# Gate and up products of up to five experts per batch as seven products over 64 channels

## Chip, cores, metric

One core of a Trainium2 chip runs the whole program. The metric is the device time of one execution in microseconds (us); lower is better. Engines: TensorE (PE, matmuls, with its weight loads as PEld), VectorE (DVE), ScalarE (ACT), GpSimd (POOL) and SyncE (SP, which here only issues DMAs). Each engine works through its own instructions strictly in program order and waits on semaphores for the others.

## What is computed

A block of linear attention and a block of eight dense experts, each between two layer norms with a residual, on 8 batches of 512 tokens with 128 channels, all in float32. The expert part is the larger one:

```python
x = x + _layernorm(attn(_layernorm(x), gamma, beta, w_qkv, w_out, b_out))
x = x + _layernorm(ffn(_layernorm(x), Wg, Wu, Wd))

def ffn(hidden, Wg, Wu, Wd):              # 8 experts, 128 channels, 512 inner
    x = hidden.reshape(-1, H)
    def expert_step(acc, w):
        wg, wu, wd = w
        h = silu(x @ wg) * (x @ wu)
        return acc + h @ wd, None
    acc, _ = scan(expert_step, zeros_like(x), (Wg, Wu, Wd))
```

## The kernel before

**Tiling of the experts.** The order of all work is written out by hand. For each batch `b` a list of units runs 32 steps; step `i` is block `f = i % 4` of 128 inner channels of expert `e = i // 4`. A step issues two matmuls, gate (L1164) and up (L1165): 128 input channels, 128 outputs, up to 512 tokens. A float32 matmul is two passes on PE, each with a weight load of its own. ACT takes the silu of the gate from PSUM (L1190), DVE multiplies it by up (L1196) into `h`. Two gate and two up banks of PSUM (`ps_gu`) take turns. All weights of gate, up and down are loaded once at the start and stay in SBUF (L116 to L125).

**Down-projection.** After the 32 steps `down_pairs` (L988) multiplies `h` with `wd`. Two blocks of 128 inner channels make a pair, two halves of the tokens and two halves of the outputs a 2x2 product that is done in Winograd's form with seven products instead of eight. `differences` (L978) makes the token-side terms of a pair on POOL with three instructions (L984 to L986); `weight_sums` (L966) makes the weight-side terms once. Each product has 64 output channels and is placed in one half of PE's columns, so two run side by side as column tiles (L1024), into the banks `accA` and `accB`. The pool `tp` has 10 buffers for `t`; the first 10 pairs get their differences during the steps, the last 6 during the down-projection.

**Around it.** `plan` (L1032) says at which step a piece of other work is issued, `meanwhile` (L1123) at which two pairs of the down-projection. While batch `b` is in its steps, the attention of batch `b+1` is finished (`context`, `values`, `stats3`, `scales3`, `residual`, `stats4`, `scales4`, `norm4`, `turn4`) and that of `b+2` begun (`load`, `stats`, `scales`, `norm`, `turn`, `affine`); `product` (L592) makes the keys of `b+2` (`k_ps`) just before the down-projection, and `softmax` follows in it. `scales` (L251) is a few small DVE instructions, then a power and a product on POOL. `turn` and `turn4` transpose blocks on DVE and pass them through DRAM (`carry_out`, one DMA; `carry_in`, four). The finished batch goes through `Last`: `turn` brings the two accumulators to tokens, `add` (L688) sums the seven products on DVE, `stats`, `scales` and `norm` make the last layer norm and store.

**Batch 0 and 7.** Batch 0 starts in pieces of one and two token blocks, so that PE has work early; its first 16 steps are run in two units. The last batch runs 24 steps whole and its last 8 in two halves with a plain down-projection, so that the end is short.

Of the kernel before, what the change touches and what calls it, by code (L numbers as in the profile page):

```python
# [9 lines left out]
F32 = mybir.dt.float32  # L10
# [6 lines left out]
def kernel(  # L17
# [60 lines left out]
    zp = ctx.enter_context(tc.tile_pool(name="zp", bufs=2))  # L78
    small = ctx.enter_context(tc.tile_pool(name="small", bufs=3))
    sgp = ctx.enter_context(tc.tile_pool(name="sgp", bufs=3))  # L80
    hp = ctx.enter_context(tc.tile_pool(name="hp", bufs=16))
    tp = ctx.enter_context(tc.tile_pool(name="tp", bufs=10))
    dram = ctx.enter_context(tc.tile_pool(name="dram", bufs=4, space=bass.MemoryType.DRAM))
    blk = ctx.enter_context(tc.tile_pool(name="blk", bufs=2))
    ps_gu = ctx.enter_context(tc.tile_pool(name="ps_gu", bufs=2, space=bass.MemoryType.PSUM))
    ps_acc = ctx.enter_context(tc.tile_pool(name="ps_acc", bufs=1, space=bass.MemoryType.PSUM))
    ps = ctx.enter_context(tc.tile_pool(name="ps", bufs=2, space=bass.MemoryType.PSUM))
# [27 lines left out]
    wg_sb, wu_sb, wd_sb = [], [], []  # L115
    for e in range(E):  # L116
        g = const.tile([P, F], F32, name=f"wg_{e}")
        nc.sync.dma_start(g, wg[e])
        u = const.tile([P, F], F32, name=f"wu_{e}")
        nc.sync.dma_start(u, wu[e])  # L120
        d = const.tile([P, NF, C], F32, name=f"wd_{e}")
        nc.sync.dma_start(d, wd[e].rearrange("(f p) c -> p f c", p=P))
        wg_sb.append(g)
        wu_sb.append(u)
        wd_sb.append(d)  # L125
# [206 lines left out]
    x2s, zTs, was, attentions, rest = {}, {}, {}, {}, []  # L332
# [225 lines left out]
    class Attention:  # L558
# [94 lines left out]
        def turn4(self):  # L653
            b = self.b
            zT = zp.tile([P, NQ, NJ, Q], F32, tag="zT", name=f"zT_{b}")
            to_channels(self.z, zT.rearrange("c a j i -> c a (j i)"), f"z_blk_{b}")
            zTs[b] = zT

    class Last:
# [28 lines left out]
        def add(self):  # L688
# [6 lines left out]
            nc.vector.tensor_tensor(u, p1, p6, ALU.add)  # L695
            nc.vector.tensor_tensor(c11, p1, p2, ALU.add)
            nc.vector.tensor_tensor(p4, p4, p4b, ALU.add)
            nc.vector.tensor_tensor(c21, u, p7, ALU.add)
            nc.vector.tensor_tensor(c12, u, p5, ALU.add)
            nc.vector.tensor_tensor(c22, c21, p5, ALU.add)  # L700
            both = q[:, 2:6].rearrange("p (s b) x -> p s b x", s=2)
            nc.vector.tensor_tensor(both, both, D[:, 0], ALU.add)
# [249 lines left out]
    LAG = 2  # L952
    FIRST = 16
    EARLY = 10
# [9 lines left out]
    ws_sb = [const.tile([P, NF // 2, 4, HALF], F32, name=f"ws_{e}") for e in range(E)]  # L964

    def weight_sums(engine, experts):  # L966

        for e in experts:
            w = wd_sb[e].rearrange("p (q k) c -> p q k c", k=2)
            a11, a21, a12, a22 = (w[:, :, k, c : c + HALF] for k in (0, 1) for c in (0, HALF))  # L970
            t = ws_sb[e]
            for i, (a, b, op) in enumerate((
                (a21, a22, ALU.add), (t[:, :, 0], a11, ALU.subtract), (a11, a21, ALU.subtract),
                (a12, t[:, :, 1], ALU.subtract),
            )):
                engine.tensor_tensor(t[:, :, i], a, b, op)

    def differences(pair):  # L978


        h = pair[0]
        t = tp.tile([P, 3, N // 2], F32, tag="t2", name="t2")
        pair.append(t)
        nc.gpsimd.tensor_tensor(t[:, 0:2], h[:, 1::2], h[:, 0:2], ALU.subtract)  # L984
        nc.gpsimd.tensor_tensor(t[:, 2], h[:, 3], t[:, 0], ALU.subtract)  # L985
        nc.gpsimd.tensor_tensor(h[:, 1], h[:, 2], t[:, 2], ALU.subtract)  # L986

    def down_pairs(b, pairs, calls):  # L988
# [4 lines left out]
        A, D = sums = [  # L993
            ps_acc.tile([P, N], F32, tag=f"acc{t}", name=f"acc{t}_{b}") for t in "AB"
        ]
        low, high = slice(0, HALF), slice(HALF, C)
        left, right = slice(0, N // 2), slice(N // 2, N)
        for two in range(0, len(pairs), 2):
            below, above = [], []
            for m, (h, t) in enumerate(pairs[two : two + 2]):  # L1000
                k = two + m
                e, pair = divmod(k, NF // 2)
                w0, w1 = wd_sb[e][:, 2 * pair], wd_sb[e][:, 2 * pair + 1]
                sm = ws_sb[e][:, pair]


                opens, closes = k == 0, k == len(pairs) - 1
# [3 lines left out]
                    (D[low, right], sm[:, 3], h[:, 3], opens, closes),  # L1011
# [3 lines left out]
                    (A[high, right], sm[:, 1], t[:, 2], opens, False),  # L1015
                    (D[high, left], sm[:, 2], t[:, 1], False, closes),
# [8 lines left out]
            late = EARLY + two // 2  # L1025
            if late < len(pairs):
                differences(pairs[late])
            for call in calls.get(two // 2, []):
                call()
        fins[b] = Last(b, sums)  # L1030

    def plan(b, lo, hi, begin):  # L1032
# [11 lines left out]
        def differ(k):  # L1044
            return lambda: differences(pairs[k])

        if b == B - 1 and begin:
            if not lo:
                at(24, lambda: fins[b].turn_both())
            else:  # L1050
                at(26, lambda: fins[b].add())
# [8 lines left out]
        elif b == 0 and begin < FIRST:  # L1060
# [8 lines left out]
            else:  # L1069
# [9 lines left out]
                for k in range(2):  # L1079
                    at(12 + 2 * k, differ(k))  # L1080
# [167 lines left out]
```

## Time and profile before

| what | us |
|---|---|
| median of 3 runs (683.97 to 684.29) | 684.22 |
| the profiled execution's span | 682.0 |
| one whole batch, 2 to 6 (183.01 to 265.78 and so on) | 82.77 |
| its down-projection (241.4 to 265.6) | 24.2 |
| POOL busy in one such batch | 52.8 |
| DVE busy in one such batch | 36.1 |
| ACT busy in one such batch | 30.7 |
| POOL busy from 241.6 to 265.7 (24.1) | 20.3 |

The span is what the profiler saw of one execution; the time of a run is 2.2 us more. A group's row gives line, engine, operation, output and inputs, shapes, the count, the busy time, the mean of one instruction in ns, and the idle time of the engine before them with what ended it. The chain of waits follows the work that ended last backwards, each time to what released it. In a timeline a row is start, length, engine, line, operation, and in brackets the idle time before it.

### The profile page before, as it was taken

The page shows a single profiled execution, that of the slowest core. Times are in us where ns is not written, and L with a number is a line of the kernel's source. Part 1 is how long each engine was busy: PE and PEld are TensorE (multiplying, and loading weights), DVE is VectorE, ACT ScalarE, POOL GpSimd, SP SyncE. Part 2 cuts the span into 40 slices and gives each one's busy share as a digit, 9 for nine tenths or more (in the row PEclk, how much of TensorE's full clock was granted, in tenths as well). Part 3 has the DMA queues.
Part 4 walks back from the last instruction along what each step waited for, and adds up shares of the span by engine and source line. Part 5 has one row for each costly group of instructions (what it writes and reads, how often), then busy time and mean ns, then how long its engine had stood idle before and what let it go on. Part 6 is the DMA issues. An engine that isn't in the chain of part 4 may idle for free.

```text
span 682.0 us, 9332 instructions
## 1 busy us (share of the span) xinstructions
PE 675.9 (99%) x3185; PEld 375.8 (55%) x3185; DVE 301.2 (44%) x806; ACT 249.3 (37%) x491; POOL 434.6 (64%) x543
## 2 busy tenths in 40 slices
PE   9999999999999999999999999999999999999997
PEld 7865565445654465544654446544465445644576
DVE  6756405554155441564325652356504545043425
ACT  5473332545035441344313443235412441033212
POOL 7599974775658576575855749557495583767501
PEclk9999999999999999999999999999999999999999
DMA  8511012010020111110111001201012000010020
GB/s 270 167 47 47 32 32 79 0 62 32 24 70 16 47 32 36 58 31 32 32 62 32 32 31 33 73 21 32 31 33 77 1 31 1 17 62 0 1 72 22
DMA packets 36815, 30.82 MB, mean 45 GB/s; under 512 B 4000, under 2 KB 28192, under 8 KB 36768
## 3 DMA queue, kind: packets, MB, share of 16 engines
q1 hardware_dynamic: 36192, 30.10, 13.8%
q8 instruction: 25, 0.41, 0.2%
q14 instruction: 22, 0.18, 0.1%
q10 hardware_dynamic: 576, 0.13, 0.1%
HBM read 18.42 MB, written 11.80 MB: 44 GB/s over the span
## 4 chain that ended last, share of the span: by engine, by line
PE 98%; DVE 0%; DMA 0%; POOL 0%; issue 0%; POOLq 0%; ACT 0%
PE g L1164 33%; PE u L1165 32%; PE accA L1024 16%; PE accB L1024 12%; PE y_ps L627 1%; PE g_ps L531 1%; PE k_ps L595 1%; PE end L905 1%; PE end_A L905 0%; DMA x<-in_L_attn_x_dram 0%; PE wa_ps L552 0%; PE m_ps L546 0%; PE c_ps L540 0%; PE end_B L905 0%; PE k_ps L397 0%; PE c_ps L432 0%
## 5 line engine op out<-in xcount | busy, mean ns | idle before, releaser
L1196 DVE TENSOR_TENSOR h<-sg,u 128x512 f32<-128x512 f32 (+2 forms) x268 | 172.9, 647 | 331.4 <-PE u L1165 310.6
L1190 ACT ACTIVATE sg<-g 128x512 f32<-128x512 f32 (+2 forms) x268 | 150.8, 564 | 338.0 <-PE g L1164 317.5
L1164 PE MATMUL g<-zT,wg 128*128 128x512 f32 (+2 forms) x568 | 267.3, 552 | 0.0
L1165 PE MATMUL u<-zT,wu 128*128 128x512 f32 (+2 forms) x568 | 266.2, 550 | 0.0
L984 POOL TENSOR_TENSOR t<-h 128x512 f32<-128x512 f32 x124 | 158.3, 1276 | 124.6 <-PE accB L1024 63.1
L1165 PEld LDWEIGHTS u<-zT,wu 128*128 128x128 f32 x568 | 107.3, 190 | 113.2 <-issue 109.3
L1164 PEld LDWEIGHTS g<-zT,wg 128*128 128x128 f32 x568 | 102.9, 190 | 95.6 <-issue 92.3
L1024 PE MATMUL accA<-h,wd 128*64 128x256 f32 x620 | 145.7, 380 | 0.0
L1024 PE MATMUL accB<-t,ws 128*64 128x256 f32 x496 | 137.8, 380 | 0.0
L1024 PEld LDWEIGHTS accA<-h,wd 128*64 128x64 f32 x620 | 84.3, 137 | 40.7 <-PE u L1165 3.8
L986 POOL TENSOR_TENSOR h<-h,t 128x256 f32<-128x256 f32 x124 | 90.8, 732 | 9.7
L985 POOL TENSOR_TENSOR t<-h,t 128x256 f32<-128x256 f32 x124 | 90.4, 729 | 9.7
L1024 PE MATMUL accA<-t,ws 128*64 128x256 f32 x248 | 73.8, 379 | 0.0
L1024 PE MATMUL accB<-h,ws 128*64 128x256 f32 x248 | 73.8, 379 | 0.0
L268 POOL TENSOR_TENSOR rstd<-ve,mhalf 128x4 f32<-128x4 f32 (+1 forms) x28 | 32.8, 1171 | 59.3 <-DVE nm L266 47.5
L1024 PEld LDWEIGHTS accB<-t,ws 128*64 128x64 f32 x496 | 67.3, 137 | 0.0
L1024 PEld LDWEIGHTS accB<-h,ws 128*64 128x64 f32 x248 | 34.0, 137 | 17.9
L1024 PE MATMUL accB<-h,wd 128*64 128x256 f32 x124 | 36.9, 379 | 0.0
L1024 PEld LDWEIGHTS accA<-t,ws 128*64 128x64 f32 x248 | 34.0, 137 | 0.0
L276 ACT ACTIVATE fn<-q,nm,rstd 128x128 f32<-128x128 f32 x28 | 11.5, 482 | 39.3 <-POOL nm L269 39.3
L276 ACT ACTIVATE x<-x,nm,rstd 128x128 f32<-128x128 f32 x56 | 22.9, 482 | 0.8 <-DVE z_blk L313 0.8
L1024 PEld LDWEIGHTS accB<-h,wd 128*64 128x64 f32 x124 | 17.0, 137 | 8.9
(207 smaller groups left out, 396.2 us busy)
## 6 DMA issues: line engine op xcount, KB each, us to landing
wg<-in_L_ffn_Wg_dram SPq DMA_DIRECT2D x8, 256.0 KB, 6.0
wu<-in_L_ffn_Wu_dram SPq DMA_DIRECT2D x8, 256.0 KB, 5.9
wd<-in_L_ffn_Wd_dram SPq DMA_DIRECT2D x8, 256.0 KB, 6.1
bounce<-f_blkA SPq DMA_DIRECT2D x8, 256.0 KB, 2.0
fA<-bounce SPq DMA_DIRECT2D x32, 64.0 KB, 2.0
bounce<-f_blkB SPq DMA_DIRECT2D x8, 256.0 KB, 2.2
fB<-bounce SPq DMA_DIRECT2D x32, 64.0 KB, 2.0
x<-in_L_attn_x_dram SPq DMA_DIRECT2D x7, 256.0 KB, 2.8
```

Of the source, the lines that this page charges most:

```text
L268: nc.gpsimd.tensor_tensor(rstd, ve, mhalf[:, :n], ALU.pow)
L276: nc.scalar.activation(d, t, AF.Identity, bias=nm[:, i : i + 1], scale=rstd[:, i : i + 1])
L531: nc.tensor.matmul(g_ps[:, :C], xh[:, j, :], ek[:, :, j * Q : (j + 1) * Q], start=(j == 0), stop=(j == NJ - 1),)
L595: nc.tensor.matmul(k_ps, w_qkv_sb[:, C : 2 * C], self.xnT, start=True, stop=True)
L984: nc.gpsimd.tensor_tensor(t[:, 0:2], h[:, 1::2], h[:, 0:2], ALU.subtract)
L985: nc.gpsimd.tensor_tensor(t[:, 2], h[:, 3], t[:, 0], ALU.subtract)
L986: nc.gpsimd.tensor_tensor(h[:, 1], h[:, 2], t[:, 2], ALU.subtract)
L1024: nc.tensor.matmul(o, w, r, start=start, stop=stop)
L1164: nc.tensor.matmul(g_ps[:, :cols], wg_sb[e][:, w], zT, start=True, stop=True)
L1165: nc.tensor.matmul(u_ps[:, :cols], wu_sb[e][:, w], zT, start=True, stop=True)
L1190: nc.scalar.activation(sg[:, :cols], g_ps[:, :cols], AF.Silu)
L1196: nc.vector.tensor_tensor(flat(h2)[:, first : first + cols], sg[:, :cols], u_ps[:, :cols], ALU.mult)
```

## The change

Experts 3 to 7 of batches 1 to 6 and experts 3 to 5 of batch 7 get gate and up by a 2x2 scheme of seven products. The 128 input channels are split in two halves of 64, the outputs (blocks `f` by twos) in two, the tokens in two halves. Gate and up are done side by side: one in rows 0 to 63 of PE, the other in rows 64 to 127 (`product`), each of 64 channels, 128 outputs and 256 tokens; a product is four such matmuls. The other experts keep the step of before.

- **Weights.** The weight-side terms are made once, in batch 0, by `start_forms` (four DMAs for each of two tiles), `form_chain` and `form_other` (three DVE instructions each, both operands in SBUF) and stored in DRAM (`forms`). Gate and up weights no longer stay in SBUF: `fetch` loads those of the next use into one of three buffers (512 KB, or 917 KB for a formed expert) when `done` says a buffer is read. `wd` is loaded in turn with them. `weight_sums` keeps three sums and overwrites a part of `wd`; the last batch loads `wd` of experts 6 and 7 again.
- **Tokens.** `turn4` writes the transposed tokens a second time, as `zd`, with eight more DMAs, so that both 64-channel halves lie in both halves of the partitions; `factors` makes the token-side terms with four DVE instructions at step 2.
- **PSUM.** One pool of four slots of two banks; `seven` uses slots 0 and 1, 2 and 3 by turns. Slot 3 is also the accumulator of the down-projection, slot 2 the attention's.
- **Between.** ACT copies three partial sums from PSUM, DVE adds, ACT takes four silus, POOL multiplies three quarters of `h` and DVE the fourth.
- **Order.** All attention work of a batch's steps is in its first 12 steps; `residual` and `stats4` to `turn4` are in the down-projection; `affine` stands behind `seven`. `add` of the last batch is on POOL, at step 5.
- **Down-projection.** It goes by quads (a whole expert). `tp` has four buffers of a quad's `t`; quads 0 and 1 get their differences at steps 6 and 10, 2 and 3 inside `seven`, 4 and 6 on POOL and 5 and 7 on DVE in the down-projection.

The core of the diff:

```diff
-    hp = ctx.enter_context(tc.tile_pool(name="hp", bufs=16))
-    tp = ctx.enter_context(tc.tile_pool(name="tp", bufs=10))
+    wp = ctx.enter_context(tc.tile_pool(name="wp", bufs=3))
+    hp = ctx.enter_context(tc.tile_pool(name="hp", bufs=8))
+    tp = ctx.enter_context(tc.tile_pool(name="tp", bufs=4))
...
+    slots = [psum.tile([P, 2, N], F32, name=f"s{k}") for k in range(4)]
...
+    def done(use):
+        del held[use]
+        fetch()
+        if wd_left:
+            fetch_wd(wd_left.pop(0))
...
+    def form_chain(e):
+        x = jobs[e][0]
+        a11, a21, a12, a22 = (columns(x, k, f) for k in (0, 1) for f in (0, 1))
+        nc.vector.tensor_tensor(a12, a21, a22, ALU.add)
+        nc.vector.tensor_tensor(a21, a11, a21, ALU.subtract)
+        nc.vector.tensor_tensor(a12, a12, a11, ALU.subtract)
+        nc.sync.dma_start(forms[e][:, : 2 * F].rearrange("p (k f) -> p k f", k=2), x)
...
+        def factors(self):
...
+            nc.vector.tensor_tensor(tz[:, 0], b22, b12, ALU.subtract)
+            nc.vector.tensor_tensor(b12, b12, b11, ALU.subtract)
+            nc.vector.tensor_tensor(tz[:, 1], b22, b12, ALU.subtract)
+            nc.vector.tensor_tensor(tz[:, 2], b21, tz[:, 1], ALU.subtract)
...
+    def differences(quad, engine=None):
+        h = quad[0]
+        t = tp.tile([P, 2, 3, N // 2], F32, tag="t4", name="t4")
+        quad.append(t)
+        sub = (engine or nc.gpsimd).tensor_tensor
+        return [
+            lambda: sub(t[:, :, 0:2], h[:, :, 1::2], h[:, :, 0:2], ALU.subtract),
+            lambda: sub(t[:, :, 2], h[:, :, 3], t[:, :, 0], ALU.subtract),
+            lambda: sub(h[:, :, 1], h[:, :, 2], t[:, :, 2], ALU.subtract),
+        ]
...
             for two_tiles in zip(below, above):
                 for o, w, r, start, stop in two_tiles:
                     nc.tensor.matmul(o, w, r, start=start, stop=stop)
-            late = EARLY + two // 2
-            if late < len(pairs):
-                differences(pairs[late])
-            for call in calls.get(two // 2, []):
+            if EARLY + e < len(quads):
+                differ(quads[EARLY + e], nc.vector if e % 2 else nc.gpsimd)
+            for call in calls.get(e, []):
                 call()
...
+        def product(bank, rows, weight, moving, start=False):
+            for q in range(2):
+                o = slice(q * N // 2, (q + 1) * N // 2)
+                for kind in sorted(range(2), key=lambda kind: rows[kind].start):
+                    r = rows[kind]
+                    nc.tensor.matmul(
+                        bank[:, kind, o], weight[r, q], moving[r], start=start and q == 0,
+                        stop=True, skip_group_check=True,
+                    )
...
+        for k, e in enumerate(experts):
+            x = Seven(k, e)
+            work7.append(x)
+            v = work7[k - 1] if k else None
+            u = work7[k - 2] if k > 1 else None
+            x.z1()
+            if v:
+                v.add22()
+            if u:
+                u.gate(u.c12)
+                u.up(u.c12, 1)
+                if k == 2:
+                    rest += differences(quads[FIRST_SEVEN])
+            x.w2()
+            x.take1()
+            if v:
+                v.z4()
+            x.add11()
+            if v:
+                v.gate(v.c22)
+                v.up(v.c22, 3)
+                v.gate21()
+            spare()
+            x.z6()
+            if v:
+                v.up21()
+            x.take6()
+            if v:
+                v.w3()
+                done(v.use)
+                v.add12()
+            x.w5()
+            x.gate(x.c11)
+            x.up(x.c11, 0)
+            spare()
+            x.z7()
+            x.take5()
+        v, u = work7[-1], work7[-2]
+        v.add22()
+        u.gate(u.c12)
+        u.up(u.c12, 1)
+        v.w3()
+        v.z4()
+        done(v.use)
+        v.gate(v.c22)
+        v.up(v.c22, 3)
+        v.add12()
+        v.gate21()
+        v.up21()
+        v.gate(v.c12)
+        v.up(v.c12, 1)
+        spare(len(rest))
...
             at(0, last("turn"))
             at(1, last("turn"))
+            at(2, attentions[b].factors)
...
+            at(5, last("add"))
             if b + 2 < B:
                 second = lambda name: lambda: getattr(attentions[b + 2], name)()
...
+                at(0, lambda: load(b + 2))
+                at(4, second("stats"))
+                at(5, second("scales"))
+                at(6, second("norm"))
+                at(8, second("turn"))
...
+            at(6, take_off(0))
+            at(10, take_off(1))
...
-        p[0] += last("add")
-        if b == 0:
-            first = attentions[1]
+        first = attentions.get(b + 1)
+        if first:
             p[0] += [first.residual]
-            p[1] += [first.stats4, first.scales4, first.norm4, first.turn4]
         if a:
             p[0] += [a.softmax]
+        if first:
+            p[1] += [first.stats4, first.scales4, first.norm4, first.turn4]
+        if b == 0:
+            for e, i in ((6, 0), (7, 3)):
+                p[i] += [partial(start_forms, e)]
+                p[i + 2] += [partial(form_chain, e), partial(form_other, e)]
         p[1] += last("stats") + last("scales")
...
         if whole:
+            if b:
+                calls = differences(quads[2])
+                experts = list(range(FIRST_SEVEN, end // NF))
+                seven(b, experts, quads, calls)
             if b + 2 < B:
+                if b:
+                    attentions[b + 2].affine()
                 attentions[b + 2].product()
-            down_pairs(b, pairs, meanwhile(b))
+            down_quads(b, quads, meanwhile(b))
```

In `seven`, `z1`, `z6`, `z7` and `z4` are products that add up in one slot, `w2`, `w5` and `w3` in the other; `take1`, `take6` and `take5` are ACT's copies of 2 x 512 elements, `add11`, `add12` and `add22` DVE's sums of a copy with a slot, `gate` the silu on ACT, `up` the product on POOL, `gate21` and `up21` the same straight from PSUM on ACT and DVE. `take_off` calls `differ` on POOL.

## Prediction

> **What bounds the kernel now.** I read the busy shares, then the chain of waits, then the groups kept apart by shape, then the timeline of one down-projection.
>
> ```profile
> PE 675.9 (99%) x3185; PEld 375.8 (55%) x3185; DVE 301.2 (44%) x806; ACT 249.3 (37%) x491; POOL 434.6 (64%) x543
> ...
> PE 98%; DVE 0%; DMA 0%; POOL 0%; issue 0%; POOLq 0%; ACT 0%
> ```
>
> TensorE (PE) is never idle and is the whole chain: PE work removed is time won, and any wait put on PE is time lost. Weight loads (PEld) lie under the matmuls. The other prices come from these groups (busy us, then mean ns of one):
>
> ```profile
> L1196 DVE TENSOR_TENSOR h<-sg,u 128x512 f32<-128x512 f32 x232 | 159.1, 687 | 322.0 <-PE u L1165 305.9 <-ACT sg L1190 16.1
> L984 POOL TENSOR_TENSOR t<-h 128x512 f32<-128x512 f32 x124 | 158.3, 1276 | 124.6 <-PE accB L1024 63.1 <-DVE h L1196 61.5
> L1190 ACT ACTIVATE sg<-g 128x512 f32<-128x512 f32 x232 | 138.0, 595 | 327.5 <-PE g L1164 307.3 <-DVE mv L257 20.1
> L985 POOL TENSOR_TENSOR t<-h,t 128x256 f32<-128x256 f32 x124 | 90.4, 729 | 9.7
> L1196 DVE TENSOR_TENSOR h<-sg,u 128x256 f32<-128x256 f32 x28 | 11.6, 419 | 8.8 <-PE u L1165 4.7 <-ACT sg L1190 3.2 <-PE z_ps L292 0.4
> L1190 ACT ACTIVATE sg<-g 128x256 f32<-128x256 f32 x28 | 10.6, 381 | 9.2 <-PE g L1164 9.0
> ```
>
> From 256 to 512 elements ACT grows by 214 ns, DVE by 268, POOL by 547; carried on to 1024 elements (estimates) ACT takes 1.02 us, DVE 1.22, POOL 2.37.
>
> PE in the down-projection of batch 2, two column tiles side by side:
>
> ```profile
> 330.25 0.14 PEld L1024 LDWEIGHTS accA<-h,wd 128*64 128x64 f32 x1
> 330.26 0.14 PEld L1024 LDWEIGHTS accB<-t,ws 128*64 128x64 f32 x1
> 330.47 0.14 PEld L1024 LDWEIGHTS accA<-h,wd 128*64 128x64 f32 x1
> 330.47 0.14 PEld L1024 LDWEIGHTS accA<-t,ws 128*64 128x64 f32 x1
> ```
>
> Both tiles load at one moment, and a new pair of passes starts every 0.216 us. Last, VectorE (DVE) and POOL where both work from SBUF, at one batch's end:
>
> ```profile
> 242.91 0.28 DVE L699 TENSOR_TENSOR q<-q,fB 128x128 f32<-128x128 f32 x1
> 243.11 1.37 DVE L700 TENSOR_TENSOR q<-q,fB 128x128 f32<-128x128 f32 x1
> 244.51 0.91 DVE L702 TENSOR_TENSOR q<-q,fB 128x256 f32<-128x256 f32 x1
> ```
>
> ```profile
> 242.99 1.33 POOL L984 TENSOR_TENSOR t<-h 128x512 f32<-128x512 f32 x1 [9.26 <-PE accB L1024]
> 244.40 0.73 POOL L985 TENSOR_TENSOR t<-h,t 128x256 f32<-128x256 f32 x1
> 245.21 0.79 POOL L986 TENSOR_TENSOR h<-h,t 128x256 f32<-128x256 f32 x1
> ```
>
> L700 has the shape of L699 and takes 1.37 us for 0.28: it ends when POOL's L984 does. A DVE instruction with two SBUF operands waits for POOL's running one. L1196, one operand in PSUM, does not.
>
> **The products (-27.4).** One step of `f` (two full matmuls, 512 columns) is four passes of 0.43 us, 1.72; an expert is 6.88. The new expert is 28 matmuls of 64 rows and 256 columns, two passes each, two row tiles at once: 28 pairs of passes. Row tiles are not in the trace. Nearest row: the column tiles' 0.216 a pair; upper bound: two 128-column weight loads one after the other, 2 x 0.190 (mean of L1164's loads) = 0.38. I take 0.216, as one 0.190 load fits under it: 6.05 an expert, 0.83 saved. Five experts in batches 1 to 6 and three in batch 7 are 33: 27.4 us.
>
> [...] The column tiles here reach 98% of the full array's rate, which is why I hold to the row.
>
> **Inside seven (+14.3).** Per expert ACT has three 1024-element copies and four gates, 5.4 us; DVE three adds and one product, 4.35; POOL three products, 3.8: each under 6.05. The tightest loop is w5, take5, add22, next z4, z6, w3, w5: 0.20 (PE's stream to ACT's start, 293.16 to 293.36) + 1.02 + 0.03 + 1.22 + 0.1 + four products of 0.864 = 6.03. It just fits; I take no stall (bounds 0 and 0.2 an expert). At the start nothing lies between: z6 waits for take1 (0.45), w5 for add11 (0.39), z7 for take6 (0.07), the next z4 for add22 (0.28). At the end only w3 lies between z7 and the last z4: add22 ends 1.61 after z7, z4 starts at 1.71, not 0.86: 0.85. Together 2.04 a batch, seven times.
>
> **Tile modes (+1.2).** From column tiles to the full array the next matmul starts 0.1 late (265.40 to 265.71 where 0.215 is usual). Two more changes in batches 1 to 5, one in 6 and 7: 12 x 0.1.
>
> **The key product (+11.5).** `affine` moves from step 30 to behind `seven`. It is last in ACT's queue: after z4 ends, gate21 (0.20 + 0.60), gate c12 (0.60) and affine itself (L583, 0.80) must pass before k_ps, 0.1 later. PE, with down_quads queued behind k_ps, idles 2.3 us, in batches 1 to 5.
>
> **Steps 0 to 11 (+2).** They now hold the attention of both later batches. ACT's norm at step 6 waits for the 8-column power (1.64) of step 5; that delays a gate so that step 9 waits some 0.4 us; five times. Upper bound 2 each. The fetches (917 KB for an expert of seven) have three experts' time, 18 us; at the 289 GB/s of the first 24.7 us one takes 3.2.
>
> **Quad 6 (+49.8).** This decides. Count from the first down matmul; each quad is 3.02 us of PE (the steps of the chain), so quad 6 is wanted at 18.1. `tp` has four buffers, so quad 4's differences wait for quad 0's products: POOL starts at 2.8 and needs 5.0 (2.37 + 1.28 + 1.28 and gaps). Behind it in POOL's queue lie the residual sum (1.27), the power and product of scales4, those of the last batch's scales, and only then quad 6. DVE holds quad 5's differences (three two-operand SBUF instructions), stats4, the transpose of turn4, then the last batch's stats.
>
> With DVE and POOL running on without holding each other: quad 4 7.8, residual 9.07, stats4 and its aggregates 10.6, power and product 11.9, four norms 13.6, transpose 14.3, last stats 15.75, their power 17.0, quad 6 17.05 to 22.05: 4.0 late. With each two-operand DVE instruction waiting for POOL's and POOL's for it: residual 10.65, stats4 begins at 11.3, power and product 14.05, transpose 16.5, power and product 19.2, then quad 7's DVE work and quad 6 by turns, to 26.4: 8.3 late. The rows show DVE waiting in full and POOL by 0.06 behind instructions of 0.28; how far POOL waits behind one of 1.22 they don't show. I take the upper end, since L986's 0.79 for 0.73 is a wait too: 8.3 in batches 1 to 6.
>
> [...]
>
> **The clock (+11.4).** The granted clock halves 2.7 us after PE's last matmul (at 680.2; the last ends at 677.5), and the first ten matmuls take 603 ns for 381. A stall of 8.3 us reaches that; restarting took some 4 us, so about 1.9 us are lost. Six times; bounds 0 and 3.4 each.
>
> **Batch 0 (+5).** Forms of experts 3 to 5: six two-operand DVE instructions each, 0.42 plus a wait of about 0.7 behind POOL, in two steps of 1.72; three PSUM pairs cover some 2.7 of the delay; I take 3 in all. Those of 6 and 7 fall beside quads 6 and 7: 2. Bounds 0 and 10.
>
> **Covered.** Formed weights' stores, the eight added DMAs for `zd` (0.35 to issue each; landed near 25, the next batch starts after 32), reloads of wd: all under PE's products. If down ran its bare 24.2 us, `zd` would come about 1 us after the batch's start, before step 2 needs it.
>
> **Sum.** -27.4 + 14.3 + 1.2 + 11.5 + 2 + 49.8 + 11.4 + 5 = +67.8. On the profiled span of 682.0: 749.8; the median lies 2.2 above the span, so 752.
>
> **Rivals.** *Queue without lock*: quad 6 waits only for its place in POOL's queue, 4.0; 25.8 less, and 3 less in batch 0: 723. For it: POOL's rows are hardly lengthened. Against: DVE's are, by a factor of five. *Quad 6 in time* (the other side): the rows of scales leave POOL free before 13.1, so that its 5.0 end by 18.1; that point decides. Quad 6, the clock, batch 0 and steps 0 to 11 then cost nothing: -0.4, 683.8, no slower, and faster if the border waits are shorter as well. Against: the chain residual to transpose took 6.5 us in batch 0 (81.6 to 88.1), and it can't start before quad 4 is through. *Weight loads in turn*: 0.38 a pair, 10.64 an expert, 4.6 x 33 more: about 900. Against: the paired loads above.
>
> **Chances.** Forecast 0.55, lock-free queue 0.25, quad 6 in time 0.12 (0.07 faster, 0.02 same, 0.03 slower), loads in turn 0.05, else 0.03. A change under 0.2% can't be told from none here. Faster 0.08, same 0.03, slower 0.89. The lowest bounds of clock, batch 0 and steps with the 4.0 give 708; the highest of all these, the loop's 0.2 an expert too, 781; a little of the third case and of a PE pass over 0.216 widens this to 700 and 785.
>
> **What would show it.** PE passes in `seven` every 0.216; PE idle before k_ps of 2.3 us with affine as releaser; PE idle before quad 6 of 4 to 9 us released by POOL, with the clock dropping there; DVE differences far over 1.2 us. If quad 6's wait is missing, or quad passes are well over 0.216, the forecast is wrong.

## The result, and the profile after

The changed kernel takes 841.89 us (median of 4 runs, 839.55 to 842.12), the one before 684.25 on the same chip: a ratio of 1.2297, interval 1.228 to 1.2314. The forecast was 752, with 700 to 785 as its range: the side was right, the size was off by 90 us. The profiled execution took 839.55, its span is 837.7 us (before 682.0): 155.7 more, where the terms summed to 67.8.

First the busy shares, the chain of waits and the granted clock, from the page of the changed kernel:

```profile
PE 719.7 (86%) x4505; PEld 462.4 (55%) x4505; DVE 423.5 (51%) x860; ACT 345.5 (41%) x590; POOL 495.0 (59%) x460
...
PEclk9998898999989999999989999899998999899999
...
PE 61%; DVE 19%; POOL 7%; ACT 6%; issue 3%; DMA 2%; SPq 1%; DVEq 0%; ACTq 0%; POOLq 0%
```

PE was 99% busy and 98% of the chain; now it idles for 118 us, and DVE holds 19% of the chain, more than POOL, at which the forecast looked. The groups by shape say where:

```profile
L1445 PE MATMUL s<-zT,w 128*128 128x512 f32 x200 | 113.0, 647 | 54.7 <-DVE h L1477 54.2
...
L1141 PE MATMUL s<-t,ws 128*64 128x256 f32 x496 | 150.1, 407 | 22.9 <-POOL t L1099 22.2 <-DVE t L1099 0.7
L1162 PE MATMUL s<-zd,w 64*128 64x256 f32 x1056 | 128.3, 380 | 3.0 <-ACT s L1203 2.1
L1162 PE MATMUL s<-tz,w 64*128 64x256 f32 x792 | 102.5, 388 | 2.6 <-ACT s L1203 1.7
```

The last column is the idle time before the group and who ended it. The new row-tile matmuls (L1162) wait for hardly anything. Quad 6 (POOL's L1099) costs 22.2 us of waiting. The largest wait, 54.2 us, stands before the gate matmul of the plain steps (L1445) and is ended by DVE's product `h` (L1477); no term of the forecast has it. With the shorter shapes of batches 0 and 7 it is 63.6 us on the page; some 45 of these are 58 waits of 0.6 to 0.9 us, and 7.46 and 4.45 are two waits for the weight sums (below). On the page of the kernel before, the gate matmul waits for nothing:

```profile
L1164 PE MATMUL g<-zT,wg 128*128 128x512 f32 (+2 forms) x568 | 267.3, 552 | 0.0
```

The same by stage, from the starts of PE's stages in the timeline. Before, a whole batch of 82.77 us is 24.2 of down-projection, 0.86 of key product, 34.4 for 20 steps of 1.72, and so 23.3 for the first 12 steps with the attention's products.

| part | forecast, us | measured, us |
|---|---|---|
| batch 0 (100.2 to 133.0) | +5 | +32.9 |
| steps 0 to 11 of batches 1 to 6 (194.9 against 6 x 23.3) | +2 | +55.1 |
| seven and key product there (213.1 against 6 x 34.4 + 5 x 0.86) | -0.1 | +2.4 |
| down-projection there: quad 6 and clock (192.7 against 6 x 24.2) | +61.2 | +47.5 |
| batch 7 (103.9 against 86.1) | -0.4 | +17.8 |
| sum | +67.7 | +155.7 |

The rows of forecast are the prediction's terms: -24.9 + 12.2 + 1.1 + 11.5 for `seven` and the key product of batches 1 to 6, 49.8 + 11.4 for the down-projection, and -2.5 + 2.0 + 0.1 for batch 7.

Of the steps' 55.1 some 7.5 are a wait of batch 1 for the weight sums (below). Batch 1's down-projection and batch 2's steps 0 to 11 as windows (length; busy us and count of PE, PEld, DVE, ACT, POOL; granted clock; DMA share; GB/s):

```profile
208.60:242.00 33.40, 29.49 (x225) 18.48 (x224) 12.42 (x30) 8.50 (x17) 18.89 (x16) 0.85 0.18 56
242.04:273.07 31.03, 25.61 (x72) 11.54 (x71) 15.81 (x45) 8.10 (x15) 11.80 (x15) 1.00 0.36 115
```

```profile
242.04 1.12 PE L1445 MATMUL s<-zT,w 128*128 128x512 f32 x2
243.00 1.02 PE L1446 MATMUL s<-zT,w 128*128 128x512 f32 x2
243.20 0.60 ACT L1471 ACTIVATE sg<-s 128x512 f32<-128x512 f32 x1 [10.08 <-PE s L1445]
244.13 0.69 DVE L1477 TENSOR_TENSOR h<-sg,s 128x512 f32<-128x512 f32 x1 [14.05 <-PE s L1446]
...
244.88 1.12 PE L1445 MATMUL s<-zT,w 128*128 128x512 f32 x2 [0.85 <-DVE h L1477]
```

In the first window PE idles 3.9 us and runs at 0.85 of its clock; in the second the clock is full and 5.4 us are idle. The second fence shows rows of the first step there and the gate of the next. Gate runs from 242.04, up from 243.00, ACT's silu and DVE's product follow, and the next step's gate starts only when that product has ended: 2.84 us for a step of 1.72, although two gate and two up banks are there.

### The profile page after: what moved, and what is told of

It reads as the page before. It is cut to its first block, busy times and chain, and to the rows that moved or that the text cites. A ratio compares the mean times of both kernels' runs of the same rounds, so it can differ in the third digit from the quotient of the medians.

```text
span 837.7 us, 12135 instructions
## 1 busy us (share of the span) xinstructions
PE 719.7 (86%) x4505; PEld 462.4 (55%) x4505; DVE 423.5 (51%) x860; ACT 345.5 (41%) x590; POOL 495.0 (59%) x460
## 3 DMA queue, kind: packets, MB, share of 16 engines
q1 hardware_dynamic: 63520, 88.57, 33.4%
## 4 chain that ended last, share of the span: by engine, by line
PE 61%; DVE 19%; POOL 7%; ACT 6%; issue 3%; DMA 2%; SPq 1%; DVEq 0%; ACTq 0%; POOLq 0%
PE s L1162 22%; PE s L1141 13%; PE s L1445 13%; PE s L1446 10%; DVE h L1477 6%; POOL rstd L352 3%; DVE t L1099 2%; ACT s L1203 2%; POOL t L1099 2%; DVE t L1100 1%; DVE h L1101 1%; ACT z L360 1%; DVE stats L332 1%; DMA Y<-in_L_ffn_Wg_dram 1%; DVE s L1216 1%
## 5 line engine op out<-in xcount | busy, mean ns | idle before, releaser
L1445 PE MATMUL s<-zT,w 128*128 128x512 f32 (+2 forms) x304 | 145.4, 560 | 67.7 <-DVE h L1477 63.6
L1477 DVE TENSOR_TENSOR h<-sg,s 128x512 f32<-128x512 f32 (+2 forms) x136 | 82.6, 608 | 220.3 <-PE s L1446 176.5
L1141 PE MATMUL s<-h,wd 128*64 128x256 f32 x744 | 188.3, 401 | 0.0
L1141 PE MATMUL s<-t,ws 128*64 128x256 f32 x496 | 150.1, 407 | 22.9 <-POOL t L1099 22.2
L1446 PE MATMUL s<-zT,w 128*128 128x512 f32 (+2 forms) x304 | 133.6, 522 | 0.0
L1162 PE MATMUL s<-zd,w 64*128 64x256 f32 x1056 | 128.3, 380 | 3.0 <-ACT s L1203 2.1
L1099 POOL TENSOR_TENSOR t<-h 128x1024 f32<-128x1024 f32 x47 | 111.0, 2361 | 32.1 <-PE s L1141 27.6
L1141 PEld LDWEIGHTS s<-h,wd 128*64 128x64 f32 x744 | 104.7, 145 | 44.8 <-issue 6.2
L1445 PEld LDWEIGHTS s<-zT,w 128*128 128x128 f32 x304 | 48.5, 191 | 127.4 <-DVE h L1477 104.7
L1162 PEld LDWEIGHTS s<-zd,w 64*128 64x128 f32 x1056 | 100.5, 187 | 24.7 <-issue 5.3
L1162 PE MATMUL s<-tz,w 64*128 64x256 f32 x792 | 102.5, 388 | 2.6 <-ACT s L1203 1.7
L1229 POOL TENSOR_TENSOR h<-s 128x512 f32<-128x512 f32 x66 | 84.3, 1278 | 13.9 <-ACT s L1225 12.9
L1446 PEld LDWEIGHTS s<-zT,w 128*128 128x128 f32 x304 | 58.0, 193 | 51.8 <-issue 49.3
L1162 PEld LDWEIGHTS s<-tz,w 64*128 64x128 f32 x792 | 72.7, 186 | 23.1 <-DVE s L1222 10.1
```

Of the source, the lines that this page charges most:

```text
L1099: lambda: sub(t[:, :, 0:2], h[:, :, 1::2], h[:, :, 0:2], ALU.subtract),
L1141: nc.tensor.matmul(o, w, r, start=start, stop=stop)
L1162: nc.tensor.matmul(bank[:, kind, o], weight[r, q], moving[r], start=start and q == 0, stop=True, skip_group_check=True,)
L1229: nc.gpsimd.tensor_tensor(self.h[:, :, i], c[:, 0], c[:, 1], ALU.mult)
L1445: nc.tensor.matmul(g_ps[:, :cols], wt[:, :F][:, w], zT, start=True, stop=True)
L1446: nc.tensor.matmul(u_ps[:, :cols], wt[:, F : 2 * F][:, w], zT, start=True, stop=True)
```

## The experiments

Theory after this: the 0.85 us are a wait for a PSUM slot. `Banks` hands out halves of slots that are one tile of two banks, and the two counters `g` and `u` are out of step by one when the whole steps begin, so that gate of step i+1 lies in the slot whose other half holds up of step i; a wait is kept for the tile, not for its half. Rival: it is the silu's buffers, of which the changed kernel has two for three. Beside this the forecast's own steps are tried: quad 6 and the holding between DVE and POOL, the key product, the weight sums.

**e1_phase: gate and up of a step in one slot.**

```diff
-    ps_gu = Banks(g=[(0, 0), (1, 0)], u=[(0, 1), (1, 1)])
+    ps_gu = Banks(g=[(0, 0), (1, 0)], u=[(1, 1), (0, 1)])
```

> The two places of the bank list for up are swapped, so that gate and up of a step lie in one slot. Theory (gate of step i+1 lies in the slot that holds up of step i, and waits until DVE has read that): the 0.85 us waits of PE behind DVE's product in steps 0 to 11 vanish, 31.0 us of steps in batch 2 become about 24, and the time falls by 7 x 7 us and some of batch 0: 780 to 795. Rival (two buffers for the gate's silu where there were three, or DVE's load in these steps): the waits stay, 842.

Measured 797.7 us, 44 less for one exchange of two pairs. Rows of the first step of batch 2 in e1, with the gate of the next:

```profile
221.55 1.13 PE L1445 MATMUL s<-zT,w 128*128 128x512 f32 x2
222.51 1.02 PE L1446 MATMUL s<-zT,w 128*128 128x512 f32 x2
223.37 1.02 PE L1445 MATMUL s<-zT,w 128*128 128x512 f32 x2
223.57 0.60 ACT L1471 ACTIVATE sg<-s 128x512 f32<-128x512 f32 x1 [10.85 <-PE s L1446]
224.20 0.69 DVE L1477 TENSOR_TENSOR h<-sg,s 128x512 f32<-128x512 f32 x1 [14.52 <-ACT sg L1471]
```

The next gate starts at 223.37, before the silu. The tile's wait is still there, but it now falls on ACT, which waits for up (L1446) instead of gate and has time for it. The changed kernel's two silu buffers are untouched here, so they don't make the wait either. By stage, batch 0 is 15.0 us shorter and batch 7 12.2, steps 0 to 11 of batches 1 and 6 13.0 together, but those of batches 2 to 5 only 0.7 to 1.1 each, where the theory had 7. There a second wait came up behind the first, here in batch 2:

```profile
236.75 0.46 POOL L809 TENSOR_TENSOR fB<-fB,fA 128x128 f32<-128x128 f32 x1 [3.76 <-DMA fB<-bounce]
...
239.20 1.65 POOL L352 TENSOR_TENSOR rstd<-ve,mhalf 128x8 f32<-128x8 f32 x1
...
241.16 1.65 ACT L360 ACTIVATE xh<-x,nm,rstd 128x128 f32<-128x128 f32 x4 [5.36 <-POOL nm L353]
...
244.07 1.22 PE L1445 MATMUL s<-zT,w 128*128 128x512 f32 x1 [4.34 <-DVE h L1477]
```

`add` of the last batch waits in POOL's queue for its transfer; the power of `scales` stands behind it, ACT's `norm` waits for that, the silu stands behind `norm`, and PE loses 4.3 us.

**e5_phase_order: e1, and `stats` and `scales` ahead of that `add`.**

```diff
-                at(4, second("stats"))
-                at(5, second("scales"))
+                at(3, second("stats"))
+                at(4, second("scales"))
```

> The bank order of the first experiment, and statistics and scales of the next but one batch one step earlier (3 and 4), so that their power stands before the sums of the last batch in POOL's queue. Theory (the one 4 us wait left in steps 0 to 11 is ACT's norm at step 6, which waits for a power that stands in POOL's queue behind sums that wait for a DMA): that wait vanishes in batches 1 to 5, the steps of batch 2 take about 24.5 us instead of 30.3, and the time falls from 797.7 to 770 to 778. Rival (ACT or DVE are short of time there whatever the order): 790 to 798.

775.45 us. Steps 0 to 11 of batch 2 fall from 31.0 to 24.5 (219.6 to 244.1). Both together win 66.4 us. In steps 0 to 11 of batches 1 to 6 they take 41.9 of the 55.1 away; 5.6 of what is left is batch 1's wait for the weight sums.

**e7_before_two_buffers: the rival with the silu's buffers, on the kernel before.**

```diff
-    sgp = ctx.enter_context(tc.tile_pool(name="sgp", bufs=3))
+    sgp = ctx.enter_context(tc.tile_pool(name="sgp", bufs=2))
```

> The kernel before, with two buffers for the gate's silu instead of three. Theory (the waits of the steps come from PSUM slots, not from these buffers): no change, 683.5 to 685.5. Rival (two buffers alone make PE wait behind DVE's product): over 690.

684.65 us against 684.37: with e1, that rival is out.

**e2_late_scales: quad 6 ahead of the last batch's power.**

```diff
-        p[1] += last("stats") + last("scales")
+        p[3] += last("stats") + last("scales")
```

> Statistics and scales of the batch before are issued after quad 7's differences instead of after the transpose of turn4. Theory (quad 6 waits for its place in POOL's queue behind their power): quad 6's differences begin right after the product of scales4, some 7 us earlier; the down-projection of batches 1 to 6 takes 25 to 28 us instead of 33.4, with no clock drop; 842 becomes 800 to 815. Rival (quad 6 waits for its buffer, or for DVE's sums alone): 835 to 845.

803.85 us, as the theory said. The down-projection of batch 1 takes 25.1 us instead of 33.4, and PE waits 0.52 in it. So quad 6's place in POOL's queue is the cause of its wait, and 38 us hang on it.

**e6_psum_operand: DVE's differences with one operand from PSUM.**

```diff
+        if engine is nc.vector:
+            p = slots[0].rearrange("p a (b x) -> p a b x", b=2)
+            return [
+                lambda: sub(t[:, :, 0:2], h[:, :, 1::2], p, ALU.subtract),
+                lambda: sub(t[:, :, 2], h[:, :, 3], p[:, :, 0], ALU.subtract),
+                lambda: sub(h[:, :, 1], h[:, :, 2], p[:, :, 0], ALU.subtract),
+            ]
```

> The changed kernel, with one operand of DVE's differences (quads 5 and 7, and as many in batch 7) taken from an idle PSUM bank of the same shape, so those terms are something else; all lengths, orders and waits stay. Theory (a DVE instruction with two SBUF operands and a POOL instruction hold each other up): DVE's three take 1.22, 0.69 and 0.69 us everywhere, POOL's third instruction of quad 4 takes 1.28 instead of 2.13 and the residual sum 1.27 instead of 1.71, quad 6 is ready 3 to 4 us sooner, and 842 becomes 815 to 825. Rival (POOL is slow there by itself, or DVE waits for something else): POOL's instructions stay as long, 838 to 842.

The terms that DVE makes are something else in this run. 815.5 us: 26 us go with the holding between DVE and POOL. The 38 of e2 and these 26 overlap, since both shorten the same wait for quad 6; they don't add up. Timeline of the changed kernel in batch 1: on DVE two differences of quad 5 and the first of quad 7, on POOL the last two of quad 4, the residual, the last batch's power and the first of quad 6:

```profile
215.90 1.87 DVE L1099 TENSOR_TENSOR t<-h 128x1024 f32<-128x1024 f32 x1 [3.56 <-PE s L1141]
217.80 1.65 DVE L1100 TENSOR_TENSOR t<-h,t 128x512 f32<-128x512 f32 x1
...
227.42 1.22 DVE L1099 TENSOR_TENSOR t<-h 128x1024 f32<-128x1024 f32 x1
...
215.42 1.27 POOL L1100 TENSOR_TENSOR t<-h,t 128x512 f32<-128x512 f32 x1
216.77 2.13 POOL L1101 TENSOR_TENSOR h<-h,t 128x512 f32<-128x512 f32 x1
218.86 1.71 POOL L728 TENSOR_TENSOR x<-x,x 128x512 f32<-128x512 f32 x1
...
227.52 1.98 POOL L352 TENSOR_TENSOR rstd<-ve,mhalf 128x4 f32<-128x4 f32 x1 [3.75 <-DVE nm L350]
...
230.10 2.34 POOL L1099 TENSOR_TENSOR t<-h 128x1024 f32<-128x1024 f32 x1
```

The same instructions in e6:

```profile
215.66 1.22 DVE L1101 TENSOR_TENSOR t<-h,s 128x1024 f32<-128x1024 f32 x1 [3.80 <-PE s L1148]
216.80 0.68 DVE L1102 TENSOR_TENSOR t<-h,s 128x512 f32<-128x512 f32 x1
...
216.53 1.28 POOL L1108 TENSOR_TENSOR h<-h,t 128x512 f32<-128x512 f32 x1
217.77 1.26 POOL L728 TENSOR_TENSOR x<-x,x 128x512 f32<-128x512 f32 x1
...
225.54 1.01 POOL L352 TENSOR_TENSOR rstd<-ve,mhalf 128x4 f32<-128x4 f32 x1 [3.74 <-DVE nm L350]
...
226.78 2.36 POOL L1106 TENSOR_TENSOR t<-h 128x1024 f32<-128x1024 f32 x1
```

Same lengths of data, one operand moved out of SBUF: DVE's second difference falls from 1.65 to 0.68 us, POOL's third from 2.13 to 1.28, and the power from 1.98 to 1.01. At 227.42 and 227.52 of the changed kernel it is DVE that holds POOL: DVE's L1099 begins first, has its 1.22, and POOL's power of 1.02 begun 0.10 later ends at 229.50, 0.86 after DVE. The holding goes both ways, and a small power pays for a large difference.

**e3_early_affine: `affine` at the first expert of `seven`.**

```diff
+            if not v and b + 2 < B:
+                attentions[b + 2].affine()
...
-                if b:
-                    attentions[b + 2].affine()
```

> affine of the next but one batch is issued after the first take1 of seven instead of behind it. Theory (PE idles before the key product for ACT's queue alone): the 1.97 us of idle time before the key product vanish in batches 1 to 5, and nothing else moves: 842 becomes 830 to 834. Rival (the idle time only moves, as the down-projection still waits for quad 6): 840 to 842.

824.88 us, 17 less, and 5 below the range expected. The wait before the key product is gone (1.97 to 1.98 in every batch of the changed kernel, released by L670), which is 2.0 in each of five batches; the down-projections are 0.5 to 1.8 shorter besides. Part of that is the clock: in the changed kernel's batch 1 the window from the key product on is the first row below, with 0.60 granted; in e3 it is the second, with 1.00:

```profile
207.33:211.60 4.27, 4.27 (x18) 2.02 (x20) 0.72 (x2) 3.54 (x7) 0.59 (x1) 0.60 0.20 73
208.14:212.41 4.27, 4.27 (x34) 2.50 (x34) 1.37 (x3) 4.07 (x8) 2.41 (x3) 1.00 0.41 123
```

The rest was not traced further.

**e4_no_form_sums: the changed kernel without the weight-side sums.**

```diff
-        nc.vector.tensor_tensor(a12, a21, a22, ALU.add)
-        nc.vector.tensor_tensor(a21, a11, a21, ALU.subtract)
-        nc.vector.tensor_tensor(a12, a12, a11, ALU.subtract)
...
-        nc.vector.tensor_tensor(a21, a21, a22, ALU.add)
-        nc.vector.tensor_tensor(a11, a21, a11, ALU.subtract)
-        nc.vector.tensor_tensor(a11, a12, a11, ALU.subtract)
```

> The sums of form_chain and form_other are left out (the weights are stored as loaded, so the experts of seven compute something else); loads and stores stay. Theory (DVE's two-operand instructions wait for POOL and for their loads at the head of DVE's queue, and the steps' products wait behind them): batch 0 ends 12 to 18 us earlier, among it the 7.5 us at the start of batch 1; 842 becomes 824 to 830. Rival (batch 0 is long because of the weights' loads or the opening): 838 to 842.

In this run the experts of `seven` compute something else. 831.09 us, 1 above the range expected. Batch 1 begins 9.5 us earlier (123.5 for 133.0); some of it is lost again to other waits in batch 1. What the sums look like in the changed kernel, DVE's timeline in batch 0 and at the start of batch 1, where the sums that were issued at the end of batch 0's down-projection stand:

```profile
74.78 1.50 DVE L196 TENSOR_TENSOR X<-X 128x256 f32<-128x256 f32 x1 [2.95 <-DMA X<-in_L_ffn_Wu_dram]
76.32 1.37 DVE L197 TENSOR_TENSOR X<-X 128x256 f32<-128x256 f32 x1
77.61 1.48 DVE L198 TENSOR_TENSOR X<-X 128x256 f32<-128x256 f32 x1
79.01 0.67 DVE L1477 TENSOR_TENSOR h<-sg,s 128x512 f32<-128x512 f32 x1
...
138.37 0.43 DVE L196 TENSOR_TENSOR X<-X 128x256 f32<-128x256 f32 x1 [7.41 <-DMA X<-in_L_ffn_Wu_dram]
```

Three sums of 0.42 take 4.2 us, since each waits for POOL's running instruction (those end at 76.01, 77.40 and 78.80, the sums at 76.28, 77.69 and 79.09), and a step's product (L1477) stands behind them. Those of expert 7 are worse: they stand in DVE's queue 7.4 us before their load is there, and batch 1's first product waits behind them; PE idles 7.46 us.

**e8_combined, e9_combined_more: all waits at once.** e8 is e5 with `affine` as in e3, `scales` as in e2, the key product between the last `w3` and `z4`, and the residual to `turn4` ahead of the first quad. e9 adds: `x` loaded at the end of the down-projection instead of at step 0 behind it, `affine` at the second expert, the residual in the epilog of `seven`, and the key maximum behind `seven`. The core of e9:

```diff
+            if k == 1 and b + 2 < B:
+                attentions[b + 2].affine()
...
+        if b + 1 < B:
+            attentions[b + 1].residual()
...
         v.w3()
+        if b + 2 < B:
+            attentions[b + 2].keys_product()
         v.z4()
...
-            p[1] += [first.stats4, first.scales4, first.norm4, first.turn4]
+            p[-1] += [first.norm4, first.turn4]
...
-        p[1] += last("stats") + last("scales")
+        p[3] += last("stats") + last("scales")
```

> The bank order, the step order of the first run of this set, affine after the first take1 and the key product between the last w3 and z4 of seven, residual to turn4 issued ahead of the first down quad, and statistics of the last batch behind quad 7's differences. Theory (these four waits are all that the batches lose): a whole batch takes 81 to 83 us instead of 99, the clock stays full from batch 2 on, and the time is 700 to 712, what is left being batch 0's forms and the opening. Rival (the row tiles or ACT, DVE and POOL inside seven cost more than PE's products, or new waits take their place): 725 or more.

> The combined kernel with the tokens of the next batches loaded at the end of the down-projection instead of at step 0, affine in the second expert of seven, the residual's norm at the end of seven, and the key maximum behind seven. Theory (the whole batch of 84.0 us in the combined run still holds the wait of the statistics for x, that of ACT for affine's tokens, and a late residual): a whole batch takes 80.5 to 82 us, and the time is 705 to 716. Rival (what is left is the price of the seven products themselves): 720 to 726.

e8 takes 724.49 us, between theory and rival; e9 712.44. A whole batch of e9 takes 81.9 us:

```profile
234.04:315.90 81.86, 80.88 (x577) 53.73 (x576) 53.14 (x96) 44.87 (x72) 63.42 (x55) 1.00 0.38 121
94.30:128.10 33.80, 26.56 (x225) 16.93 (x225) 15.59 (x30) 7.47 (x15) 15.92 (x13) 0.90 0.60 181
```

The first window is a whole batch, 0.9 us less than the 82.77 before. The second is batch 0's down-projection: 33.8 us, where the changed kernel takes 26.0 and the kernel before 24.3. The sums of expert 6 stand 10.95 us in DVE's queue before their load is there, quad 7's differences behind them, and PE waits 7.2 us for these (in e10, which moves the sums, it takes 24.3).

**e10_forms_spread, e11_forms_later, e12_no_sums: the sums one by one.** e10 is e9 with one sum a step instead of three, and earlier loads into four buffers; the differences of batch 0's quads move by a few steps too. e11 is e10 with the sums of experts 3, 4 and 5 later, and the loads for 5; e12 is e10 without the sums, so that it computes something else. From e10 to e11:

```diff
                 at(7, partial(start_forms, 3))
-                forms_at(3, 10, 11, 12, 13, 14, 15)
...
-            at(20, partial(start_forms, 5))
-            forms_at(4, 19, 20, 21, 22, 23, 24)
-            forms_at(5, 25, 26, 27, 28, 29, 30)
+            forms_at(3, 16, 17, 18, 19, 20, 21)
+            at(22, partial(start_forms, 5))
+            forms_at(4, 22, 23, 24, 25, 26, 27)
+            forms_at(5, 26, 27, 28, 29, 30, 31)
```

> The same, with the weight forms' DVE instructions spread one to a step from batch 0's second unit to batch 1's step 9, and their loads issued earlier into five buffers. Theory (batch 0 is long because the forms' instructions stand in threes at the head of DVE's queue, each waiting for POOL or for its load): batches 0 and 1 lose their waits of 8, 7 and 5.5 us, and the time falls by 12 to 20 us against the run before it in this set, to 685 to 700. Rival (DVE and POOL have no room for the forms in batch 0 wherever they stand): less than 6 us.

> e10 with the weight-side sums of expert 3 begun six steps later (step 16 instead of 10), those of expert 4 three and of expert 5 one step later. Theory: e10's two PE waits in batch 0 (9.36 and 2.94 us) arise only because a sum stands in DVE's queue before its load has landed (54.5 us), since SP issued the load late; behind the landing both waits go and the time falls from 709.9 to 696 to 702 us. Rival: the sums hold the steps wherever they lie, since each waits for POOL's running instruction: then less than 5 us are won, 705 or more.

> e10 with the weight-side sums left out (their loads and the stores remain; the formed weights are then not the sums). Theory: what the sums cost in e10 is the two waits and little more, so 694 to 699 us; still above the 684 of the kernel before, so that even free sums would not make this order of the change pay. Rival: the loads and stores themselves hold SP's queue and the fetches behind it, and the time stays above 704.

e10 missed: 709.88 us, within the rival's bound. Its DVE timeline shows one new wait:

```profile
44.48 0.42 DVE L1522 TENSOR_TENSOR h<-sg,s 128x256 f32<-128x256 f32 x1 [1.38 <-ACT sg L1516]
54.53 0.53 DVE L203 TENSOR_TENSOR X<-X 128x256 f32<-128x256 f32 x1 [9.62 <-DMA X<-in_L_ffn_Wu_dram]
54.98 0.41 DVE L1522 TENSOR_TENSOR h<-sg,s 128x256 f32<-128x256 f32 x1
```

SP began to issue the loads for these sums only at 46.54, behind a carry and a fetch in its queue, and the awaited one at 48.05. e11 moves the sum behind the landing:

```profile
54.93 0.65 DVE L203 TENSOR_TENSOR X<-X 128x256 f32<-128x256 f32 x1
56.14 0.69 DVE L1522 TENSOR_TENSOR h<-sg,s 128x512 f32<-128x512 f32 x1 [0.57 <-ACT sg L1516]
56.75 1.32 DVE L205 TENSOR_TENSOR X<-X 128x256 f32<-128x256 f32 x1
57.99 0.68 DVE L1522 TENSOR_TENSOR h<-sg,s 128x512 f32<-128x512 f32 x1
```

e11 takes 697.76 us, e12 697.82: the sums are nearly free once each lies behind its load and alone in its step, even at 1.3 us for a sum of 0.42. Not quite: e11 reaches batch 7 1.9 us later (603.2 for 601.3), and e12 loses 1.3 of that there at a lower clock (0.87 for 0.93 in `seven`). e11 is the best version found, 144 us below the changed kernel, and still 1.0199 (1.0169 to 1.0228) of the kernel before. Its span of 696.7 is 14.7 over before: +10.6 in batch 0 (110.8 for 100.2, of which 3.0 are the later opening, 18.5 for 15.5), +0.8 in batch 1, -4.2 in batches 2 to 6 and +7.5 in batch 7. No version that beats the kernel before was found; what is left in batches 0 and 7 was not taken apart.

## Why the prediction was right or wrong

- **Products (-27.4): held.** Passes of `seven` start every 0.216 us. An expert takes 6.15 where 6.05 was said: the loop over w5, take5, add22 and z4, at 6.03 in the forecast, is the bound by a little. The rival of weight loads in turn is out.
- **Inside seven (+14.3), tile modes (+1.2), key product (+11.5): held** as a sum with the products, to 2.4 us over six batches. The key product waits 1.97 for the 2.3 forecast, released by ACT as said.
- **Quad 6 (+49.8) and the clock (+11.4): the mechanism held, the size was 14 too large, and that only because two errors partly cancel.** Quad 6's place in POOL's queue and the holding between DVE and POOL were both right, as e2 (38 us) and e6 (26 us) show. Quad 6's differences began 21.5 us after batch 1's first down matmul (208.60 to 230.10), where the forecast has 26.4 less their 5.0. PE's wait was over-counted: the forecast let it wait for all three differences, 8.3, and PE goes on behind the first, after 3.7; that is 22.2 in six batches for 49.8. The clock was under-counted: it is at half from 232.5 to 238.8, which is 3.2 us lost for the 1.9 of the forecast; in the six batches it is 2.8 to 3.2 each, some 18 for 11.4. The upper bound of 3.4 each was the author's; no row of before shows it. The other 7 of the 47.5 were not taken apart.
- **Steps 0 to 11 (+2): the step that failed.** It priced the attention's late power at 0.4 us a batch and put the PSUM layout, which the diff shows as one pool of four slots of two banks, at nothing. These steps cost 55.1 in batches 1 to 6, and the slot wait runs through the plain steps of batches 0 and 7 too. e1 and e5 show it: freed of the slot wait and of the power's, the kernel is 66 us faster, and 41.9 of the 55.1 are gone. The power's way to PE (POOL, ACT's norm, silu, gate) was in the forecast; that it stands behind `add`, which waits for its transfer, was not, and with the slots freed that wait is 4.3 us for 0.4. How the 41.9 divide between the two can't be said, since the power's order was not tried with the old slots. The slots could have been seen in the diff: a slot is one tile, and the pair of counters decides which halves share one.
- **Batch 0 (+5): under-sized, with its mechanism right, but the larger part is another.** Sums waiting for POOL, and steps behind them, were in the forecast; without the sums (e4) batch 0 ends 9.5 us earlier. Not in it were the slot wait, 15.0 us of batch 0 in e1 (118.0 for 133.0), where the forecast counts the PSUM pairs as a cover of 2.7, and the opening 3.7 us later. Loads that land after their sums are due were not in it either; the one for expert 7 (7.41 us) falls into batch 1's steps.
- **Batch 7 (-0.4): +17.8.** Its 12 steps take 30.9 us, as in the others, and its tail from the last 8 steps on 34.2 for 26.4; with e1's slots 21.4 and 28.5. So 15.2 of the 17.8 are the slot wait; e1 gives 3.0 back in batch 7's `seven`, 23.6 for 20.5.
- **Range.** Its bounds were those of the priced terms. A part of the diff without any term, the layout of PSUM, had no bound in it.

That POOL is held too, on which the 8.3 of quad 6 stood, was an estimate from 0.79 us for 0.73; e6 shows it: with one operand of DVE's differences in PSUM, DVE's second falls from 1.65 to 0.68 us and POOL's third from 2.13 to 1.28. So the rival without lock, in which DVE and POOL don't hold each other, is out. Row tiles, for which before had no row, show no loss where two run side by side: 0.216 a pair is half of the 0.43 of a full pass of twice the columns. The forecast's 98% for the column tiles is over 99% by the same rows, 0.215 to 0.216.

## What to carry to other kernels

When a change joins buffers that were separate into one tile, write out which instruction holds which tile at each step, for a wait on half of it is a wait on all of it: here the order of two bank pairs was worth 44 us. An instruction that waits for a transfer or another engine should be put into a strictly ordered queue behind the point where its input lands, since everything behind it pays (7.4 and 9.6 us of DVE's queue here). And a scheme that saves 4 us of products in a batch of 82.8 has to hide its whole side work: freed of its waits it kept 0.9 of them, and in e11 batch 0 with its set-up costs 10.6 more where batches 2 to 6 give 4.2 back.

## What the runs showed of the hardware

- In batch 1's down-projection of the changed kernel two instructions of POOL that started while DVE ran one with two SBUF operands were held: a power of 1.02 us took 1.98, a difference of 1.28 took 2.13. The other way round three sums of DVE of 0.42 us took 1.37 to 1.50 in batch 0. Not every row shows it: DVE's second difference at 228.67 took its 0.69 us while that power was still running.
- A wait of PE of 1.97 us, before the key product, took the clock to 0.60 to 0.67 for the next 4.3 us in some batches and left it at 1.00 in others: 1 of 5 in the changed kernel, 4 of 5 in e1, 2 of 5 in e2, 1 of 5 in e4, 3 of 5 in e5, 4 of 5 in e6, so 15 of 30. Waits of 0.85 in the steps left it at 1.00. In the changed kernel it goes with where the wait lies: in its clock record the nine drops between 78 and 724 us begin whole multiples of 3.41 us apart. On that grid, the stretches around the key product of batch 1 and of batch 5:

```profile
204.70:208.11 3.41, 1.44 (x9) 0.53 (x6) 1.35 (x2) 2.78 (x7) 2.62 (x3) 1.00 0.51 148
208.11:211.53 3.42, 3.42 (x15) 1.72 (x16) 0.69 (x1) 2.75 (x5) 0.00 (x0) 0.50 0.02 5
604.06:607.47 3.41, 1.80 (x10) 0.83 (x12) 1.32 (x2) 3.10 (x7) 1.73 (x2) 1.00 0.51 154
607.47:610.88 3.41, 3.41 (x35) 2.25 (x32) 0.83 (x3) 2.06 (x3) 1.19 (x1) 1.00 0.00 0
```

  With 1.97 us of idling inside one stretch the clock is at 0.50 in the next; with 1.61, the rest of the wait being in the stretch before, it stays at 1.00. Around the key products of batches 2 to 4 no stretch of the grid has more than 1.26 us of idling, and the clock stays at 1.00 there too.
- Two row tiles of 64 channels, float32 and 256 columns, start every 0.216 us in the changed kernel's `seven` (L1162), weight loads of 0.187 included.
